# Folding an image's normalisation into the projection's weights and a bias, and a third buffer for a tile, in a four-layer scan and attention kernel

## The chip, the core and the metric

The kernel runs on one core of one Trainium2 chip. The core has five engines that run beside each other, each in its own program order: TensorE (PE; loads of its stationary operand are shown as PEld), VectorE (DVE), ScalarE (ACT), GpSimd (POOL) and SyncE (SP), which here only issues DMAs. The metric is the device time of one execution, in microseconds (us); lower is better.

## The reference

The input is four images of 64 x 64 positions with 96 channels. Layers 0 and 1 are a two-dimensional selective scan; layers 2 and 3 are linear attention and a quantised feed-forward network on the tokens. The change lies in layers 0 and 1. Cut to what matters, such a layer is:

```python
def _gn(v, G=32, eps=1e-5):                    # one mean and variance per image and group of 3 channels
    ...
    return ((g - m) / jnp.sqrt(s + eps)).reshape(v.shape)
...
xz = jnp.einsum('bhwc,ec->bhwe', x, in_proj_w)           # x is _gn(x)
xx, z = jnp.split(xz, 2, axis=-1)
xc = jax.lax.conv_general_dilated(xc, conv_w, (1, 1), [(1, 1), (1, 1)], ..., feature_group_count=E) + conv_b
xc = jax.nn.silu(xc)
xs = jnp.stack([x_hw, x_wh, x_hw[..., ::-1], x_wh[..., ::-1]], axis=1)
x_dbl = jnp.einsum('bkdl,kcd->bkcl', xs, x_proj_weight)
dts, Bmat, Cmat = jnp.split(x_dbl, [R, R + N], axis=2)
delta = jax.nn.softplus(jnp.einsum('bkrl,kdr->bkdl', dts, dt_projs_weight) + dt_projs_bias)
# scan over 4096 positions in 4 directions: h = exp(delta * A) * h + delta * B * u;  y = sum_n C * h
# then a layer norm, times silu(z), the projection out_proj_w, and the residual
```

## The kernel before, in words

`body` runs four phases, each one layer for a pair of images: layer 0 for pairs 0 and 1, then layer 1 for pairs 0 and 1. After them `token_layers` does layers 2 and 3. A phase has three parts.

- `prepare` (L151) computes everything the scan reads and writes it to DRAM: `delta` (split into three bf16 parts), `du` (delta times u), `bc` (B and C) and `ud` (u times the sum of Ds).
- `scan_phase` (L469) runs the scan, in an order written out by hand, from those DRAM tiles.
- `finish` (L546) puts the four directions together, normalises, gates, projects and adds the residual.

`run` (L699) runs `prepare` of one phase beside `finish` of the phase before: both are generators, and for each `yield` of `prepare`, `ph.beside` steps of `finish` are taken (1.0, then 0.6, then 1.25). The first `prepare` has no `finish` beside it. The scan of a phase uses all eight PSUM banks and starts when both are through. Outside `scan_phase` nothing is ordered by hand: a scheduler orders each engine's instructions from the program order, its dependences and the buffers that come free, and tile pools hand out the buffers (`bufs` of a tile says how many; a new tile waits for the oldest one's last reader).

Inside `prepare`:

- The statistics of both images come first (L186 to L209). `ph.gs[:, i]` holds, for image `i` and each of 96 channels, the mean of its group (column 0) and one over the standard deviation (column 1).
- `convolve` (L231) runs for image 0 alone, and then, as the generator `other`, for image 1 beside the `steps` of image 0. It goes over two halves `h` of the 192 inner channels. For each half it takes eight slices of the image: load of `rawi` (L242, two buffers, 96 x 512), the normalisation in place on DVE (L247: subtract the mean, multiply by the scale), the projection on PE (L251) into a PSUM bank named `c` (two buffers, shared with `steps`), and the eviction by ACT (L254) into the padded image `xp`, which has one buffer. Then eight chunks of a 3 x 3 depthwise convolution: tap 0 on ACT (L266), taps 1 to 8 on DVE (L268), and Silu with a bias on ACT (L271). Then `xu` (L276) is written to `ud` (L282). The margin of `xp` is set to zero (L239).
- `steps` (L284) runs for both images `i`, eight chunks `c` and two directions `k`, so 32 times in a preparation. Each time PE projects the 96 x 512 chunk (L291), ACT evicts it (L294 and L295), and PE projects to delta for two items, the direction forwards and backwards (L308, PSUM tile `d`, two buffers). Then for each of the two items: ACT takes Softplus into `dl` (L316) and casts it to bf16 (L317); DVE multiplies by u into `du_sb` (L318) and subtracts the cast from `dl` (L319); POOL casts the rest (L322); DVE subtracts that (L323). The results leave by the DMAs of L321 (two copies of `du`) and L324 (`parts` to `delta`). The tiles `dl`, `parts` and `du_sb` have two buffers each, from the pool `steps`.

All DMAs are issued by SP, in order. The lines that the change touches are L235 to L257 and L313.

Of the kernel before, what the change touches and what calls it, by code (L numbers as in the profile page):

```python
# [9 lines left out]
F32 = mybir.dt.float32  # L10
# [3 lines left out]
AF = mybir.ActivationFunctionType  # L14
ALU = mybir.AluOpType
# [7 lines left out]
C = 96  # L23
E = 192
# [5 lines left out]
TC = 512  # L30
# [25 lines left out]
def scan_view(t, k, c):  # L56


    part, half = t.ap[0], t.ap[1]
    if k == 0:  # L60
        off, steps = TC * c, (HW, 1)
    elif k == 1:
        off, steps = ROWS * c, (1, HW)
    elif k == 2:
        off, steps = L - 1 - TC * c, (-HW, -1)
    else:
        off, steps = L - 1 - ROWS * c, (-1, -HW)
    return bass.AP(t.tensor, t.offset + off, [part, half, [steps[0], ROWS], [steps[1], HW]])


def view(t, off, *dims):

    return bass.AP(t.tensor, t.offset + off, [t.ap[0]] + [list(d) for d in dims])


def rows(t):

    if len(t.shape) == 2:
        return t.rearrange("p (r w) -> p r w", w=HW)
    return t.rearrange("p h (r w) -> p h r w", w=HW)  # L80
# [50 lines left out]
class Scans:  # L131
# [99 lines left out]
    def convolve(self, ph, i, x, xc, in_w, taps, conv_b, dsum):  # L231


        nc = self.nc
        with self.tc.tile_pool(name="conv", bufs=1) as cp:  # L235
            for h in range(2):
                xp = cp.tile([C, PAD, PAD], F32, name="xp")
                for edge in (xp[:, 0, :], xp[:, PAD - 1, :], xp[:, 1 : PAD - 1, 0], xp[:, 1 : PAD - 1, PAD - 1]):
                    nc.vector.memset(edge, 0.0)  # L239
                for hl in range(8):  # L240
                    raw = cp.tile([C, TC], F32, name="rawi", bufs=2)
                    nc.sync.dma_start(  # L242
                        raw.rearrange("c (a p) -> c a p", p=64), x[:, hl * 8 : hl * 8 + 8, i]
                    )
                    if hl % 2 == 0:
                        yield
                    nc.vector.tensor_scalar(  # L247
                        raw, raw, ph.gs[:, i, 0:1], ph.gs[:, i, 1:2], ALU.subtract, ALU.mult
                    )
                    ps = self.bank()  # L250
                    nc.tensor.matmul(  # L251
                        ps[:C], in_w[:, h * C : (h + 1) * C], raw, start=True, stop=True
                    )
                    nc.scalar.copy(  # L254
                        view(xp, (1 + hl) * PAD + 1, (1, 8), (8 * PAD, 8), (8, 8)),
                        ps[:C].rearrange("c (a h w) -> c a h w", a=8, h=8),
                    )  # L257
                for c in range(NC):
                    yield
                    acc = xc[:, h, c * TC : (c + 1) * TC]  # L260
                    for tap in range(9):
                        dy, dx = divmod(tap, 3)
                        src = xp[:, ROWS * c + dy : ROWS * (c + 1) + dy, dx : dx + HW]
                        w = taps[:, h, tap : tap + 1]
                        if tap == 0:
                            nc.scalar.activation(rows(acc), src, AF.Copy, scale=w)  # L266
                        else:
                            nc.vector.scalar_tensor_tensor(  # L268
                                rows(acc), src, w, rows(acc), ALU.mult, ALU.add
                            )  # L270
                    nc.scalar.activation(acc, acc, AF.Silu, bias=conv_b[:, h : h + 1])  # L271
                for hl in range(8):
                    if hl % 2 == 0:
                        yield
                    xu = cp.tile([C, 8, 64], F32, name="xu", bufs=2)
                    nc.scalar.activation(  # L276
                        xu.rearrange("c w (a b) -> c w a b", b=8),
                        view(xc[:, h], hl * HW, (1, 8), (8 * HW, 8), (8, 8)),
                        AF.Copy,
                        scale=dsum[:, h : h + 1],  # L280
                    )
                    nc.sync.dma_start(ph.ud[:, h, 8 * hl : 8 * hl + 8, i], xu)  # L282

    def steps(self, ph, sp, xc, xp, dt_w, i, k, c):  # L284


        nc, cst = self.nc, self.cst
        u = scan_view(xc, k, c)
        ps = self.bank()
        for h in range(2):  # L290
            nc.tensor.matmul(rows(ps[:XD2]), xp[:, k, h], u[:, h], start=h == 0, stop=h == 1)  # L291
        xd = sp.tile([XD2, TC], F32, name="xd")

        nc.scalar.activation(xd[:XD], ps[:XD], AF.Identity, bias=cst.one_row[:XD])  # L294
        nc.scalar.activation(  # L295
            xd[64:], view(ps[64:XD2], TC - 1, (-1, TC)), AF.Identity, bias=cst.one_row[64:]
        )
        yield
        both = []
        for back in range(2):  # L300
            at = 64 * back
            g, cc = 2 * (k + 2 * back) + i, NC - 1 - c if back else c
            nc.sync.dma_start(ph.bc[cc][:, g], xd[at : at + 2 * NS])
            both.append((g, cc, scan_view(xc, k + 2 * back, cc), self.p_d.tile([C, 2, TC], F32, name="d")))
        for m in range(2):
            for back, (_, _, _, ps) in enumerate(both):
                part = slice(64 * back + 2 * NS, 64 * back + XD)
                nc.tensor.matmul(  # L308
                    ps[:, m], dt_w[part, k, m * C : (m + 1) * C], xd[part], start=True, stop=True
                )  # L310
        yield
        for g, cc, u, ps in both:
            delta = sp.tile([C, 2, TC], F32, name="dl")  # L313
            parts = sp.tile([C, NP16, 2, TC], BF16, name="parts")
            du = sp.tile([C, 2, TC], F32, name="du_sb")
            nc.scalar.activation(delta, ps, AF.Softplus)  # L316
            nc.scalar.copy(parts[:, 0], delta)  # L317
            nc.vector.tensor_tensor(rows(du), rows(delta), u, ALU.mult)  # L318
            nc.vector.tensor_tensor(delta, delta, parts[:, 0], ALU.subtract)  # L319
            for copy in range(2):  # L320
                nc.sync.dma_start(ph.du[cc][copy, g, :E].rearrange("(h e) t -> e h t", h=2), du)  # L321
            nc.gpsimd.tensor_copy(parts[:, 1], delta)  # L322
            nc.vector.tensor_tensor(parts[:, 2], delta, parts[:, 1], ALU.subtract)  # L323
            nc.sync.dma_start(  # L324
                ph.delta[cc][g].rearrange("n (h q) t -> q (n h) t", h=2),
                parts.rearrange("q n h t -> q (n h) t"),
            )
            yield
# [660 lines left out]
```

## Time and profile before

Three runs took 11978.79, 11985.35 and 12007.12 us; the median is 11985.35 us. The profile is of one more execution.

| what | value |
|---|---|
| the profiled execution's own time | 11973.68 us |
| its span, first to last instruction | 11971.9 us |
| mean granted TensorE clock | 0.826 of full speed |
| busy DVE / PE / POOL / ACT / PEld | 10052.3 / 8659.6 / 7465.3 / 7321.2 / 4597.6 us |
| first preparation | 0 to 725 us |
| the three other preparations, with a finish beside each | 2595 to 3465, 5310 to 6180, 8030 to 8900 us |
| the four scans | 725 to 2595, 3465 to 5310, 6180 to 8030, 8900 to 10769 us |
| last finish and the token layers | 10769 to 11972 us |

How to read the lines that follow. A group is: line, engine, operation, output <- input with shapes, count | busy us, mean ns of one | idle us of that engine just before these instructions, and what ended that idle time. A timeline row is: start us, duration us, engine, line, operation, output <- input, count of merged instructions, and in brackets how long the engine had been idle and what released it. A row of windows is a stretch, its length and the busy time of each engine in it. An fp32 matmul is two records on PE. Engine names with a q (SPq, DVEq) are the engine's queue: instructions that only issue or wait.

The granted clock in the preparations is 0.64 to 0.66 on the mean, in the scans 0.90 to 0.91. GpSimd is nearly idle in a preparation: 107 us of work in the first.

### The profile page before, as it was taken

The page shows a single profiled execution, that of the slowest core. Times are in us where ns is not written, and L with a number is a line of the kernel's source. Part 1 is how long each engine was busy: PE and PEld are TensorE (multiplying, and loading weights), DVE is VectorE, ACT ScalarE, POOL GpSimd, SP SyncE. Part 2 cuts the span into 40 slices and gives each one's busy share as a digit, 9 for nine tenths or more (in the row PEclk, how much of TensorE's full clock was granted, in tenths as well). Part 3 has the DMA queues.
Part 4 walks back from the last instruction along what each step waited for, and adds up shares of the span by engine and source line. Part 5 has one row for each costly group of instructions (what it writes and reads, how often), then busy time and mean ns, then how long its engine had stood idle before and what let it go on. Part 6 is the DMA issues. An engine that isn't in the chain of part 4 may idle for free.

```text
span 11971.9 us, 337755 instructions
## 1 busy us (share of the span) xinstructions
PE 8659.6 (72%) x144960; PEld 4597.6 (38%) x144960; DVE 10052.3 (84%) x10351; ACT 7321.2 (61%) x12109; POOL 7465.3 (62%) x2316
## 2 busy tenths in 40 slices
PE   3567777765767777765777777766677777777777
PEld 1124444442334444442334444433234444444333
DVE  6679999987769999987769999986769999993667
ACT  4556666655556666655556666654557666662556
POOL 0169999960149999970149999970139999990000
PEclk8579999986679989886679999986668999998887
DMA  3677777764677777765677777764677777763110
GB/s 98 185 244 254 255 252 252 252 206 138 197 231 255 254 256 257 257 216 143 193 226 256 258 257 252 258 219 136 199 221 258 255 254 250 254 232 125 18 21 11
DMA packets 952267, 2501.23 MB, mean 209 GB/s; under 512 B 324494, under 2 KB 607220, under 8 KB 819316
## 3 DMA queue, kind: packets, MB, share of 16 engines
q1 hardware_dynamic: 950772, 2479.63, 62.8%
q8 instruction: 1142, 18.71, 0.7%
q14 instruction: 353, 2.89, 0.1%
HBM read 1965.42 MB, written 513.80 MB: 207 GB/s over the span
## 4 chain that ended last, share of the span: by engine, by line
DMA 56%; PE 12%; DVE 11%; SPq 10%; ACT 5%; issue 4%; POOL 2%; POOLq 0%; DVEq 0%; ACTq 0%
DMA h<-du 52%; SPq L399 9%; DVE xc L268 4%; PE f L594 2%; POOL parts L322 2%; PE d L308 1%; PE c L291 1%; DVE parts L323 1%; DVE dl L319 1%; DVE du_sb L318 1%; DMA yk<-y 1%; PE c L251 1%; PE f L603 1%; PE f L674 1%; PE f L660 1%
## 5 line engine op out<-in xcount | busy, mean ns | idle before, releaser
L409 POOL TENSOR_TENSOR h<-h,b 128x1536 f32<-128x1536 f32 x2048 | 7021.1, 3461 | 533.5 <-DMA h<-du 191.9
L426 DVE TENSOR_TENSOR_SCAN h<-a,carry,h 128x512 f32<-128x512 f32 x5376 | 6345.7, 1259 | 174.6 <-POOL h L409 171.9
L419 ACT ACTIVATE a<-a,a_col 128x512 f32<-128x512 f32 x6144 | 4031.0, 664 | 1856.7 <-PE a L415 1830.9
L444 PEld LDWEIGHTS y<-h,cw 128*32 128x32 f32 x131072 | 2786.7, 128 | 3501.2 <-issue 1310.9
L444 PE MATMUL y<-h,cw 128*32 128x48 f32 x131072 | 3660.1, 266 | 527.3 <-DVE h L426 211.6
L415 PE MATMUL a<-dlt,rep 72*128 72x512 bf16 x6144 | 2526.8, 422 | 1302.3 <-DVE h L426 1212.9
L322 POOL CAST parts<-dl 96x1024 bf16<-96x1024 f32 x256 | 416.1, 1630 | 2793.0 <-DVE dl L319 2587.0
L456 ACT COPY d<-y 128x384 f32<-128x384 f32 x2048 | 979.8, 478 | 475.0 <-PE y L444 429.8
L426 DVE TENSOR_TENSOR_SCAN h<-a,h 128x512 f32<-128x512 f32 x768 | 868.3, 1200 | 165.5 <-ACT a L419 142.6
L415 PEld LDWEIGHTS <-rep 72*128 72x128 bf16 x6144 | 487.2, 98 | 829.0 <-issue 587.8
L308 PE MATMUL d<-xd,dt_w 7*96 7x512 f32 x1024 | 631.7, 905 | 237.5 <-ACT dl L316 149.6
L268 DVE SCALAR_TENSOR_TENSOR xc<-xp,conv_w,xc 96x512 f32<-96x512 f32 x1024 | 713.8, 756 | 54.8 <-ACT xc L266 38.9
L826 POOL MEMSET tn<- 1x4096 f32 x8 | 27.8, 3507 | 862.3 <-PE pa L846 515.1
L316 ACT ACTIVATE dl<-d 96x1024 f32<-96x1024 f32 x256 | 258.4, 1018 | 449.5 <-DVE parts L323 429.1
L318 DVE TENSOR_TENSOR du_sb<-dl,xc 96x1024 f32<-96x1024 f32 x256 | 416.2, 1633 | 116.7 <-ACT dl L316 73.0
L291 PE MATMUL c<-xc,x_proj 96*103 96x512 f32 x512 | 452.3, 1024 | 82.1 <-ACT xc L271 42.7
L594 PE MATMUL f<-yk,perm 128*128 128x384 f32 x1024 | 429.6, 564 | 95.4 <-DMA yk<-y 72.8
L251 PE MATMUL c<-rawi,in_w 96*96 96x512 f32 x256 | 206.0, 915 | 397.0 <-DVE rawi L247 312.1
L319 DVE TENSOR_TENSOR dl<-dl,parts 96x1024 f32<-96x1024 f32 x256 | 309.6, 1217 | 210.8 <-ACT parts L317 209.3
L323 DVE TENSOR_TENSOR parts<-dl,parts 96x1024 bf16<-96x1024 f32 x256 | 329.1, 1292 | 160.4 <-POOL parts L322 158.0
L308 PEld LDWEIGHTS d<-xd,dt_w 7*96 7x96 f32 x1024 | 171.8, 222 | 642.9 <-ACT dl L316 229.7
L361 ACT ACTIVATE cw<-c,gmask 128x256 f32<-128x256 f32 x512 | 286.0, 570 | 116.4 <-DMA dlt<-delta 58.1
(116 smaller groups left out, 5802.0 us busy)
## 6 DMA issues: line engine op xcount, KB each, us to landing
h<-du SPq DMA_DIRECT2D x1024, 768.0 KB
h<-du SPq DMA_DIRECT2D x2048, 384.0 KB
du<-du_sb SPq DMA_DIRECT2D x512, 384.0 KB
delta<-parts SPq DMA_DIRECT2D x256, 576.0 KB
dlt<-delta SPq DMA_DIRECT2D x512, 288.0 KB
y<-d SPq DMA_DIRECT2D x2048, 48.0 KB
yk<-y SPq DMA_DIRECT2D x256, 384.0 KB
ud<-xu SPq DMA_DIRECT2D x128, 192.0 KB
```

The source lines that it names most:

```text
L268: nc.vector.scalar_tensor_tensor(rows(acc), src, w, rows(acc), ALU.mult, ALU.add)
L291: nc.tensor.matmul(rows(ps[:XD2]), xp[:, k, h], u[:, h], start=h == 0, stop=h == 1)
L308: nc.tensor.matmul(ps[:, m], dt_w[part, k, m * C : (m + 1) * C], xd[part], start=True, stop=True)
L322: nc.gpsimd.tensor_copy(parts[:, 1], delta)
L399: self.nc.sync.dma_start(u.h[32 * first : 32 * (first + quarters), e : e + n].rearrange("p e t -> p (e t)"), source.rearrange("a g e t -> ...
L409: self.nc.gpsimd.tensor_tensor(h, h, b, ALU.mult)
L415: self.nc.tensor.matmul(u.a[n], self.cst.rep[:, h], u.dl[:, e], start=True, stop=True)
L419: self.nc.scalar.activation(u.a[n], u.a[n], AF.Exp, scale=u.ph.a_col[:, at : at + 1])
L426: self.nc.vector.tensor_tensor_scan(u.h[:, n], u.a.pop(n), u.h[:, n], 0.0 if u.c == 0 else u.ph.carry[:, at : at + 1], ALU.mult, ALU.add,)
L444: self.nc.tensor.matmul(view(u.y[32 * j : 32 * j + 32], l2 * EB, (8 * EB, 4), (1, EB)), u.ph.cw[u.c][:, l1, 8 * j + l2], view(u.h, 64 * l1 ...
L456: self.nc.scalar.copy(u.d[:, :, :, l1], u.y[:, : 32 * EB].rearrange("p (t h x) -> p t h x", t=4, h=2))
L594: nc.tensor.matmul(ps[:, : 4 * C].rearrange("p (w v e) -> p w v e", w=4, v=nv), cst.perm[:, k], view(t, off, (sw if k < 2 else -sw, 4), (1 ...
```

## The change

For each image `convolve` now first makes a scaled copy of the projection's weights, `in_ws`: row c (an input channel) times the scale of channel c. The mean's share is computed once: the scaled weights times the vector of means, on PE, one column for each half, negated on DVE into `shift`. The slices are no longer normalised: PE projects the loaded slice as it is with the scaled weights, and ACT's eviction adds `shift` as a per-partition bias (Identity with a bias in place of a copy). The tile `dl` gets three buffers in place of two, which takes another 4 KB of each of its partitions. `finish` still normalises its own slices for z (L652) as before.

```diff
         with self.tc.tile_pool(name="conv", bufs=1) as cp:
+            gs = ph.gs[:, i]
+            scaled = cp.tile([C, E], F32, name="in_ws")
+            nc.vector.tensor_scalar_mul(scaled, in_w, gs[:, 1:2])
+            shift = cp.tile([C, 2], F32, name="shift")
+            for h in range(2):
+                ps = self.bank()
+                nc.tensor.matmul(
+                    ps[:C, :1], scaled[:, h * C : (h + 1) * C], gs[:, 0:1], start=True, stop=True
+                )
+                nc.vector.tensor_scalar_mul(shift[:, h : h + 1], ps[:C, :1], -1.0)
             for h in range(2):
                 xp = cp.tile([C, PAD, PAD], F32, name="xp")
...
-                    nc.vector.tensor_scalar(
-                        raw, raw, ph.gs[:, i, 0:1], ph.gs[:, i, 1:2], ALU.subtract, ALU.mult
-                    )
                     ps = self.bank()
                     nc.tensor.matmul(
-                        ps[:C], in_w[:, h * C : (h + 1) * C], raw, start=True, stop=True
+                        ps[:C], scaled[:, h * C : (h + 1) * C], raw, start=True, stop=True
                     )
-                    nc.scalar.copy(
+                    nc.scalar.activation(
                         view(xp, (1 + hl) * PAD + 1, (1, 8), (8 * PAD, 8), (8, 8)),
                         ps[:C].rearrange("c (a h w) -> c a h w", a=8, h=8),
+                        AF.Identity,
+                        bias=shift[:, h : h + 1],
                     )
...
-            delta = sp.tile([C, 2, TC], F32, name="dl")
+            delta = sp.tile([C, 2, TC], F32, name="dl", bufs=3)
```

In the changed program every later line number is higher by 9 (L251 is L258, L254 is L261, L308 is L317, L316 is L325, L317 is L326, L323 is L332). The order of instructions in the two built programs, which tells no times, differs on the engines in `prepare`: where both convolutions are through, ACT had for each step two evictions and then Softplus, cast, Softplus, cast; now it has two evictions, cast, Softplus, Softplus, cast. The built programs hold 273 and 270 loads of ACT's tables. The order on DVE in that place is the same in both, and so is every engine's order in the scans.

## The prediction

> **What bounds the kernel now.** I read the chain that ended last, then the windows by stage, then the groups by line, and at last the timeline of two stretches of the first preparation. All times are in us.
>
> The page's chain, by engine and by line:
>
> ```profile
> DMA 56%; PE 12%; DVE 11%; SPq 10%; ACT 5%; issue 4%; POOL 2%; POOLq 0%; DVEq 0%; ACTq 0%
> DMA h<-du 52%; SPq L399 9%; DVE xc L268 4%; PE f L594 2%; POOL parts L322 2%; PE d L308 1%; PE c L291 1%; DVE parts L323 1%; DVE dl L319 1%; DVE du_sb L318 1%; DMA yk<-y 1%; PE c L251 1%; PE f L603 1%; PE f L674 1%; PE f L660 1%
> ```
>
> The 52% is the scan, and the change doesn't touch it. What it touches (L247, L251, L254, L316 to L323) lies in `prepare`. The windows cut the span into the first preparation, a scan, and the second preparation (each row: the stretch, its length, busy time of PE, PEld, DVE, ACT, POOL, clock, DMA share, GB/s):
>
> ```profile
> 0.00:725.00 725.00, 360.50 (x462) 98.17 (x463) 462.58 (x535) 325.33 (x359) 106.58 (x69) 0.66 0.56 158
> 725.00:2595.00 1870.00, 1433.72 (x34042) 811.47 (x34041) 1801.76 (x1533) 1286.54 (x2285) 1754.91 (x512) 0.91 0.72 251
> 2595.00:3465.00 870.00, 561.05 (x1678) 263.53 (x1679) 573.24 (x804) 423.17 (x519) 106.71 (x67) 0.66 0.61 175
> ```
>
> No engine is full in a preparation: DVE, the busiest, works 64% and 66%. So a preparation is made of dependences, and the four of them (725 and three of 870) are 3335 of 11972. That is the field.
>
> **The rows to cost with.** The removed normalisation and the eviction that gets a bias:
>
> ```profile
> L254 ACT COPY xp<-c 96x512 f32<-96x512 f32 x128 | 140.5, 1111 | 222.8 <-PE c L251 222.5
> ...
> L247 DVE TENSOR_SCALAR rawi<-rawi,gs 96x512 f32<-96x512 f32 x128 | 68.0, 539 | 166.5 <-DMA rawi<-in_x 98.6 <-DMA rawi<-x 67.2
> ```
>
> 128 instructions go, 68.0 of DVE time, and with them 166.5 in which DVE stood at L247 for a load while later work queued behind. The eviction stays at 128, and so do its wait for PE and its writes.
>
> **Normalisation, first image (nothing of `steps` runs yet).** First preparation, up to 62.6: the projection goes in rounds of two, each a load of 2.4 to 2.5, L247 0.55, PE 2.0, because `rawi` has two buffers. Three reloading rounds lose 0.55 + 0.1: 1.9. The first matmul, at 40.96, stands behind L247, which stands on DVE behind the statistics of the other image; it can start at about 38 once the weights are scaled: 3. Two L247 at 102 and 103 sit between the taps (L268), which DVE issues without a gap: 0.9. Between the halves (104.7 to 131.9, DVE nearly idle) the chain passes `xu`, its stores, the last `rawi` load (3.3), L247 (0.56), PE (2.0). The first two projections no longer wait for DVE, and the built program issues one more `rawi` load ahead of the `xu` stores: between 0.6 and 5.9 (a whole round), I take 4. Sum 10. In the other three, the first projection waits for nothing but the scale (no gain) and SP issues the last `rawi` loads late: 1.5 in the rounds, 1.1 in the taps, 4.4 between the halves (0.5 + 0.5 + 0.5 of L247 on the chain and half a round): 7 each.
>
> **Normalisation, second image (beside `steps`).** Here L247 costs more than its 0.54, since it queues on DVE behind the delta work. From the timeline of the first preparation:
>
> ```profile
> 217.34 3.16 DVE L323 TENSOR_TENSOR parts<-dl,parts 96x1024 bf16<-96x1024 f32 x2 [0.94 <-POOL parts L322]
> 220.43 0.99 DVE L247 TENSOR_SCALAR rawi<-rawi,gs 96x512 f32<-96x512 f32 x2
> 221.06 1.99 PE L251 MATMUL c<-rawi,in_w 96*96 96x512 f32 x2 [8.60 <-DVE rawi L247]
> ...
> 239.75 0.99 DVE L247 TENSOR_SCALAR rawi<-rawi,gs 96x512 f32<-96x512 f32 x2
> 240.39 1.99 PE L251 MATMUL c<-rawi,in_w 96*96 96x512 f32 x2 [10.46 <-DVE rawi L247]
> ```
>
> PE waits 8.6 and 10.5 for an L247 behind L318, L319 and L323. Without it PE needs only the load, and the taps, for which DVE idles 8.2 just before 229.7, start earlier by at most those 19. Late is then the load, the two PSUM banks and the eviction. Bounds: 16 x 0.54 = 8.6 if only DVE time counts, 35 if the second half gains as much as the first. I take 19. In the other three, finish work fills PE and DVE (PE waits for L247 62 in all in that stage, against 128 in the first), so 12 each.
>
> **Added work.** For each image two matmul pairs of one column (row L198: 0.30 a record, so 1.2), one scaling of 96x192 (row L338, 128x192: 0.24) and two negations (row L208: 0.15). The scaling waits for the statistics and stands ahead of the taps on DVE only when DVE idles (194 in the first preparation). PE holds the projection behind the two pairs: 1.0 a preparation on the path, inside the 3 above. The first eviction also waits for its negation, ready before ACT has finished the statistics (39.9), so nothing queued behind it on ACT is held. The eviction's bias is a pointer: row L295 with one, 39x512 from PSUM, 0.682; row L681 without, 96x512, 0.582. So +0.1 each, 3.2 of ACT a preparation; ACT is 45% to 49% busy there, and about 1 is on the path between halves, inside the 4. If ACT's cover were gone, 128 x 0.1 = 13. Table loads in the built programs: 273 and 270, 4 less ACT time, nothing on the path.
>
> **The third `dl` buffer.** Where both convolutions are done (about 500 to 700), a step with its two items A and B:
>
> ```profile
> 629.20 1.04 ACT L317 CAST parts<-dl 96x1024 bf16<-96x1024 f32 x1
> 629.22 3.72 PE L308 MATMUL d<-xd,dt_w 7*96 7x512 f32 x4 [0.47 <-ACT dl L316]
> 630.27 1.22 DVE L319 TENSOR_TENSOR dl<-dl,parts 96x1024 f32<-96x1024 f32 x1 [1.08 <-ACT parts L317]
> ...
> 633.56 1.22 DVE L323 TENSOR_TENSOR parts<-dl,parts 96x1024 bf16<-96x1024 f32 x1 [0.93 <-POOL parts L322]
> ...
> 634.88 1.02 ACT L316 ACTIVATE dl<-d 96x1024 f32<-96x1024 f32 x1 [4.64 <-DVE parts L323]
> ...
> 636.86 1.22 DVE L319 TENSOR_TENSOR dl<-dl,parts 96x1024 f32<-96x1024 f32 x1 [2.08 <-ACT parts L317]
> ...
> 639.27 1.22 DVE L323 TENSOR_TENSOR parts<-dl,parts 96x1024 bf16<-96x1024 f32 x1 [1.19 <-POOL parts L322]
> 640.42 1.91 DVE L318 TENSOR_TENSOR du_sb<-dl,xc 96x1024 f32<-96x1024 f32 x1
> 640.59 1.02 ACT L316 ACTIVATE dl<-d 96x1024 f32<-96x1024 f32 x1 [2.47 <-DVE parts L323]
> ```
>
> The period is one closed loop: L319 to L323 of A 4.51, Softplus and cast 2.08, L319 to L323 of B 3.63, Softplus and cast 2.22; sum 12.44, and 13.12 in every other step, where L318 reads u across rows (1.9 in place of 1.22). ACT issues Softplus, cast, Softplus, cast. In the built changed program it issues cast of A, two Softplus, cast of B: the cast of A no longer stands behind a Softplus, but the cast of B still does, behind one that takes the buffer freed by A's L323. So 2.08 stays, and 2.22 becomes the L318 it had covered (1.25 or 1.94): 24.3 in place of 25.6 for two steps, 0.62 a step. 14 steps: 9 in the first preparation; in the others, with finish work between, 6 each. Earlier, where L316 waits for L323 too (45 of 156 in the first), 3 and 2.
>
> Next late would be PE: eight L308 records at 0.93 and four L291 at 0.93, 11.2 a step, at a granted clock of 0.50:
>
> ```profile
> 560.00:620.00 60.00, 52.08 (x57) 13.67 (x58) 38.52 (x29) 24.60 (x29) 15.72 (x10) 0.50 0.78 227
> ```
>
> The Trainium skill (TensorE: Matmul & The Clock Gate, Part 1) says the clock is binary and that some 3.4 us of sustained work raise it to full. By that rule PE's step would cost 5.6 and could bind nothing. The row disagrees: 87% busy, 7.4 on end at 629 to 636, and 0.50 throughout. I keep 11.2. DMA, 0.78 busy at 12.8, has its floor at 10.
>
> **Sum.** First preparation 10 + 19 + 9 + 3 = 41; the others 7 + 12 + 6 + 2 = 27, three times 81: 122 in all. The profiled execution took 11973.7 (span 11971.9); less 122, 11851.7. The median of the runs is 11.7 above it: 11863.
>
> **Rivals.** (1) *The loops open wider*: the delta loop falls to PE's 11.2 (1.6 a step in place of 0.62, over 14 x 4 steps 55 more) and the second image reaches its upper bound (40 more): 11768. For it, the idle engines; against it, the built order on ACT. 15%. (2) *It was hidden anyway*: loads, SP's order and finish work are as late as L247 was, and only the first image's gains and some DVE time remain, 45: 11940. For it, 166.5 of L247's idle time was a load's doing. 18%. (3) *Slower, by ACT's new order*: B's cast now stands behind the second Softplus, which needs the last L308 of its step; where PE is late, each step's DVE chain starts one L308 pair and one Softplus later, 1.86 + 1.02 = 2.9. It decides once PE ends L308 after A's L323. PE is full for long in the last three preparations (100% of 3248 to 3276). Half of some 78 such steps cost 113, less 76 for the convolution: 12022. Against it, PE's loop (10.96) is shorter than 12.2 where I can follow it. 10%.
>
> **Numbers.** The forecast has 57%. The measurement tells 0.3% (36) from no change, so faster ends at 11949. Faster: 57 - 2, 15, and 10 of the second rival's 18: 0.80; same: 0.12; slower: 0.08. The range 11765 to 11955 leaves out the slower rival, the low half of the first, and the top of the second.
>
> **What would show it.** Right: L251 (L258) never waits for DVE, the gap between the halves of the first image falls from 27 to about 23, the taps of the second image start before 230, Softplus in pairs every 12.2, the scans unchanged at 1845 to 1870. Wrong: L258 waiting as long for its load, casts waiting behind Softplus, or a period still at 12.8, or PE's clock rising in the steps.

## The result, and the profile after

Four runs of the changed kernel took 11874.15 to 11923.01 us, median 11887.4; four of the kernel before 11978.79 to 12007.12, median 11984.52. The ratio is 0.9918 (95% interval 0.9898 to 0.9937): 97 us less, where 122 were forecast. A second measurement, with the kernel before taken again beside it, gave 0.9905 (0.9892 to 0.9919). The profiled execution is the slowest of the four (11923.01), 51 below the profiled one of before, since its scans are 42 longer in sum. A scan is counted from its first to its last multiplication by B on POOL (L418, L409 before), and a preparation is what lies ahead of it:

| profiled execution | preparations | sum | scans | sum |
|---|---|---|---|---|
| before | 725.0, 866.2, 862.7, 867.5 | 3321.4 | 1870, 1856, 1850, 1866 | 7443 |
| after | 710.2, 837.6, 838.6, 842.5 | 3228.9 | 1880, 1871, 1869, 1866 | 7485 |

The preparations lost 92.5, about what the medians say. The scans, which the change leaves as they were, took 7443 to 7512 in the 14 profiled executions of this study, and before's is the lowest. So I compare preparations, and use the medians for totals.

The chain of the changed kernel, by engine and by line:

```profile
DMA 57%; PE 12%; DVE 11%; SPq 10%; ACT 5%; issue 3%; POOL 2%; POOLq 0%; DVEq 0%; ACTq 0%
```

It is the same chain: the scan's loads. The windows show where the time went: the first preparation, a scan, and the second preparation:

```profile
0.00:710.00 710.00, 327.87 (x470) 99.14 (x471) 446.50 (x509) 327.46 (x359) 104.38 (x68) 0.65 0.58 161
710.00:2590.00 1880.00, 1437.56 (x34042) 811.68 (x34041) 1802.49 (x1533) 1288.62 (x2285) 1754.98 (x512) 0.90 0.72 250
2590.00:3428.00 838.00, 537.95 (x1686) 260.89 (x1687) 555.18 (x778) 422.89 (x517) 109.78 (x66) 0.65 0.63 181
```

The groups, kept apart by shape, of the lines that were L251, L254, L316 and L317:

```profile
L326 ACT CAST parts<-dl 96x1024 bf16<-96x1024 f32 x256 | 265.4, 1041 | 146.8 <-DMA delta<-parts 145.6
L325 ACT ACTIVATE dl<-d 96x1024 f32<-96x1024 f32 x256 | 257.7, 1018 | 348.6 <-DVE parts L332 259.2 <-PE d L317 87.2 <-DVE xo L696 1.2
L258 PE MATMUL c<-rawi,in_ws 96*96 96x512 f32 x256 | 195.5, 874 | 241.3 <-ACT xp L261 101.6 <-DMA rawi<-in_x 84.5 <-DMA rawi<-x 48.0
L261 ACT ACTIVATE xp<-c,shift 96x512 f32<-96x512 f32 x128 | 152.5, 1205 | 140.3 <-PE c L258 139.8
```

The projection had stood idle 312.1 for L247; now it stands 101.6 for the eviction and 132.5 for its loads (48.2 before). Softplus waited 429.1 for L323; now 259.2 for the same and 87.2 for PE. The cast's wait for the stores of `parts` rose from 99.2 to 145.6. The bias costs 94 ns an eviction (1111 to 1205), the 0.1 of the forecast.

Where each preparation gained, from the taps' and the delta work's instructions in the trace. The taps are the nine products of the convolution. Each column is the change of a stage's own length, after less before, with the forecast in brackets; the 3 and the 2 that the forecast gave to earlier steps of the `dl` loop stand with the second image. The last stage runs to the scan's first multiplication:

| preparation | to the end of the first image's taps | second image's taps | from there to the last L332 | tail | sum |
|---|---|---|---|---|---|
| first | -7.4 (forecast -10) | +0.8 (-22) | -9.3 (-9) | +1.2 | -14.7 |
| second | -7.0 | -24.8 | +3.1 | +0.1 | -28.6 |
| third | -3.5 | -20.7 | +2.1 | -2.0 | -24.1 |
| fourth | -6.4 | -23.5 | +6.3 | -1.4 | -25.0 |
| mean of these three | -5.6 (-7) | -23.0 (-14) | +3.8 (-6) | -1.1 | -25.9 (-27) |

The first preparation fell short by 26. The others met their 27, but from other terms than I summed. One execution's columns carry a few us of chance: in a second profiled execution of the changed kernel the +3.8 was -0.4.

### The profile page after: what moved, and what is told of

Its sections match the earlier page's. It is cut to its first block, busy times and chain, and to the rows that moved or that the text cites. A ratio compares the mean times of both kernels' runs of the same rounds, so it can differ in the third digit from the quotient of the medians.

```text
span 11921.2 us, 337611 instructions
## 1 busy us (share of the span) xinstructions
PE 8549.8 (72%) x144992; PEld 4586.7 (38%) x144992; DVE 9991.8 (84%) x10247; ACT 7335.1 (62%) x12106; POOL 7480.2 (63%) x2316
## 4 chain that ended last, share of the span: by engine, by line
DMA 57%; PE 12%; DVE 11%; SPq 10%; ACT 5%; issue 3%; POOL 2%; POOLq 0%; DVEq 0%; ACTq 0%
DMA h<-du 53%; SPq L408 9%; DVE xc L277 4%; PE f L603 2%; POOL parts L331 2%; PE d L317 1%; DVE dl L328 1%; PE f L683 1%; PE c L300 1%; DVE du_sb L327 1%; PE f L694 1%; DVE parts L332 1%; DMA yk<-y 1%; PE f L669 1%; PE f L612 1%
## 5 line engine op out<-in xcount | busy, mean ns | idle before, releaser
L418 POOL TENSOR_TENSOR h<-h,b 128x1536 f32<-128x1536 f32 x2048 | 7020.9, 3461 | 574.0 <-DMA h<-du 229.6
L317 PE MATMUL d<-xd,dt_w 7*96 7x512 f32 x1024 | 532.0, 885 | 263.6 <-ACT dl L325 141.2
L327 DVE TENSOR_TENSOR du_sb<-dl,xc 96x1024 f32<-96x1024 f32 x256 | 409.9, 1607 | 123.6 <-ACT dl L325 67.2
L325 ACT ACTIVATE dl<-d 96x1024 f32<-96x1024 f32 x256 | 257.7, 1018 | 348.6 <-DVE parts L332 259.2
L332 DVE TENSOR_TENSOR parts<-dl,parts 96x1024 bf16<-96x1024 f32 x256 | 326.2, 1280 | 170.0 <-POOL parts L331 168.8
L317 PEld LDWEIGHTS d<-xd,dt_w 7*96 7x96 f32 x1024 | 160.0, 216 | 586.5 <-ACT xd L303 200.1
L258 PE MATMUL c<-rawi,in_ws 96*96 96x512 f32 x256 | 195.5, 874 | 241.3 <-ACT xp L261 101.6
```

What stands on the lines that cost most here:

```text
L317: nc.tensor.matmul(ps[:, m], dt_w[part, k, m * C : (m + 1) * C], xd[part], start=True, stop=True)
L418: self.nc.gpsimd.tensor_tensor(h, h, b, ALU.mult)
```

## The experiments

All figures are ratios to the kernel before on the same chip, from five rounds, with an interval of 0.0012 to 0.0016 to each side (0.001 is 12 us). "Preparations" is the sum of the four in the profiled execution; before it is 3321. No kernel leaves work out.

| kernel | ratio (median, us) | preparations | the first |
|---|---|---|---|
| changed kernel again | 0.9905 (11903) | 3217 | 709 |
| fold alone | 0.9955 (11963) | 3266 | 722 |
| three `dl` alone | 0.9943 (11954) | 3258 | 712 |
| changed, 3 `rawi` | 0.9876 (11873) | 3174 | 685 |
| changed, `rawi` loads on GpSimd | 0.9851 (11839) | 3146 | 678 |
| the same, no fold | 0.9889 (11881) | 3181 | 688 |
| 4 `dl`, no fold | 0.9920 (11915) | 3225 | 702 |
| changed, loads on GpSimd, 3 `rawi` | 0.9846 (11835) | 3137 | 669 |
| the same, no fold | 0.9838 (11824) | 3130 | 675 |
| changed, loops of L317 exchanged | 0.9946 (11944) | 3254 | 727 |
| 3 `dl`, 3 `rawi`, no fold | 0.9912 (11911) | 3215 | 692 |
| fold, loads on GpSimd, 4 `dl` | 0.9804 (11775) | 3099 | 666 |

**The parts alone.** The fold without the buffer, and the buffer without the fold:

```diff
-            delta = sp.tile([C, 2, TC], F32, name="dl", bufs=3)
+            delta = sp.tile([C, 2, TC], F32, name="dl")
```

> The fold alone; dl keeps its two buffers. By the prediction's sum the fold was worth 86 of the 122 (29 in the first preparation, 19 in each other) and this is 86 below the kernel before. My theory after the result: in the second image L258 got the load to wait for in place of L247, the fold keeps only the first image's gain (7 in the first preparation, the taps of the second image at most 8 earlier) and this is 40 to 65 below the kernel before. Rival: the two parts need each other, and alone each brings under 25.

> The third dl buffer alone; the normalisation stays on DVE. By the prediction 36 below the kernel before (12 in the first preparation, 8 in each other), with a step of 12.2 in place of 12.8 where both convolutions are through. My theory after the result: 9 in the first preparation, 10 to 15 in each other, 35 to 55 below. Rival: with L247 still between the delta work on DVE, the buffer brings under 20.

The fold brings 54 (forecast 86; my second guess, 40 to 65, holds), the buffer 68 (forecast 36; above my second guess of 35 to 55). Alone they add up to 122; together they gave 97 and 114, which the intervals do not tell from 122. The preparations, at 55 and 63 alone and 92 and 104 together, say that the parts overlap somewhat. In the first preparation the fold brings 2.6 and the buffer 12.8. The fold's first image ends 8 earlier there, and its second image then takes 4 longer than before. That is the term to explain.

**What took L247's place.** The timeline of the changed kernel at the start of the second image, first preparation, the same place as the prediction's rows from 217 to 240 (the last row below is of the kernel before):

```profile
221.07 1.99 PE L258 MATMUL c<-rawi,in_ws 96*96 96x512 f32 x2 [1.11 <-DMA rawi<-in_x]
...
226.31 0.30 SPq L333 DMA_DIRECT2D delta<-parts  x1
...
229.86 0.55 SPq L333 DMA_DIRECT2D delta<-parts  x1
...
230.50 9.43 SPq L252 DMA_DIRECT2D rawi<-in_x  x3
237.60 1.99 PE L258 MATMUL c<-rawi,in_ws 96*96 96x512 f32 x2 [14.54 <-DMA rawi<-in_x]
...
240.87 8.13 DVE L277 SCALAR_TENSOR_TENSOR xc<-xp,conv_w,xc 96x512 f32<-96x512 f32 x12 [9.63 <-ACT xp L261]
...
243.56 6.80 DVE L268 SCALAR_TENSOR_TENSOR xc<-xp,conv_w,xc 96x512 f32<-96x512 f32 x10 [2.81 <-ACT xp L254]
```

The row of 237.60 is the eighth slice of the half. Its buffer is that of the sixth, whose matmul ended at 211.3, so SP could have issued its load then; but the stores of L330 and L333 stand ahead of it in SP's order and wait for the delta work on DVE and POOL. SP issued the load at 230.50, and PE got the slice at 237.60; why it was 7.1 on its way isn't settled. In the kernel before, the load went out at 228.54, the matmul ran at 240.39, and it seemed to have waited 10.46 for L247. The second image's first tap on DVE came at 229.7 in both kernels; it doesn't need the eighth slice. The taps that do started at 240.87, with DVE idle 9.63 for that slice's eviction, against 243.56 before: of the 10.46, 2.7 were gained. Two ways to take the load out of that place, a further buffer, or another queue with the same buffers:

```diff
-                    raw = cp.tile([C, TC], F32, name="rawi", bufs=2)
+                    raw = cp.tile([C, TC], F32, name="rawi", bufs=3)
```

> The changed kernel with a third rawi buffer, so that a load can be issued a slice ahead, before SP reaches the stores that it stood behind. Theory (the load is what is late next in the second image): L258's wait for loads, 133 in all in the changed kernel, falls below 60, the second image's taps of the first preparation start 5 to 15 earlier, and the time is 15 to 45 below the changed kernel. Rival (the delta work on DVE and ACT sets the pace beside the second image, the load only fills its gaps): within 10 of the changed kernel.

```diff
-                    nc.sync.dma_start(
+                    nc.gpsimd.dma_start(
                         raw.rearrange("c (a p) -> c a p", p=64), x[:, hl * 8 : hl * 8 + 8, i]
                     )
```

> The changed kernel with the rawi loads issued by GpSimd's queue in place of SP's, buffers as they are: a load then waits for its buffer and for GpSimd's casts (L331), not for the stores that stand ahead of it on SP. Theory (SP's order holds the load): as with a third buffer, 15 to 45 below the changed kernel. Rival 1 (the load isn't what limits): within 10. Rival 2: the loads' waits hold GpSimd's casts of the delta work behind them, and the kernel is 10 to 40 above the changed one.

Both are faster than the changed kernel: 0.0029 to 0.0042 below it, or 35 to 50, and 0.0054 to 0.0067, or 65 to 80, by its two measurements. The queue's gain is above the range I gave. The first preparation loses 24 and 31 more, and its second image's first tap comes at 207.9 and 216.8. With the third buffer that is 22 earlier, where I had thought 5 to 15; 9 of it come from the first image, whose rounds of loads it shortens as well. The row for the GpSimd queue:

```profile
210.82 0.78 POOL L252 DMA_DIRECT2D rawi<-in_x  x1
...
213.10 1.34 PE L258 MATMUL c<-rawi,in_ws 96*96 96x512 f32 x2
```

The issue takes 0.78 of GpSimd between two casts, and L258 no longer waits for the load. One expectation failed: with three buffers L258's wait for loads didn't fall below 60, it was 184. 129 of that are four waits of 30 to 33, one in each preparation, between the halves of the second image (the changed kernel has one there too, of 29.20). SP's rows of that kernel in the first preparation show the reason:

```profile
327.87 1.38 SPq L333 DMA_DIRECT2D delta<-parts  x1
...
337.03 4.11 SPq L330 DMA_DIRECT2D du<-du_sb  x2
341.25 0.59 SPq L333 DMA_DIRECT2D delta<-parts  x1
341.94 10.14 SPq L252 DMA_DIRECT2D rawi<-in_x  x4
```

The last four loads of the next half stand behind the stores, however many buffers are free; PE gets the first at 349.75. With the loads on GpSimd that sum is 57, and the gap between those halves of the first preparation falls from 55 (328.6 to 383.9) to 30 (311.9 to 341.5). The Trainium skill (DMA: Bandwidth & Descriptors, "Issuing engine by pattern") gives simple loads to SP, and calls the path that SP uses generally faster. The trace agrees: in the first image's rounds PE waits 1.0 to 1.2 for SP's loads and 1.9 to 2.0 for GpSimd's. Here the place in the queue's order mattered more than the path.

**Is the fold worth more once the load is out of the way?** Kernels without the fold beside those with it:

> The kernel before with the third dl buffer and with its rawi loads on GpSimd's queue; no fold. Beside the run that has the fold as well (0.985 of the kernel before) it gives the fold's worth with the load out of the way. Theory: the fold's gain was taken up by the load's place in SP's order, so without that place it is worth about what the prediction's sum said, 86 (29 in the first preparation, 19 in each other), and this kernel is at 0.991 to 0.993. Rival: the loads by GpSimd bring their gain by themselves, with L247 or without; then this kernel is at 0.987 to 0.989, and the fold is worth 50 or less here too.

> The kernel before with three dl buffers, the rawi loads on GpSimd's queue and three rawi buffers; no fold. It stands beside the kernel that has all this and the fold (0.9846 of the kernel before; first preparation 669). With the load well ahead, PE's waits for L247 are all DVE's. If L247 behind the delta work is then what is late, the fold is worth more here than the 45 that it was worth with two rawi buffers: 60 to 90, this kernel at 0.990 to 0.992. If the convolution's taps on DVE are the limit of the second image, L247 costs little more than its own time: the fold is worth 20 to 45, this kernel at 0.986 to 0.9885.

> The kernel before with three dl and three rawi buffers, all loads on SP; no fold. With the loads on GpSimd and three rawi buffers the fold was worth nothing (0.9838 without it, 0.9846 with it). If a third rawi buffer does the same as the fold (both take L247 out of the round of load, normalisation, projection and next load), this kernel is where the same with the fold is, 0.986 to 0.989, and below the changed kernel (0.9905 to 0.992). If the loads' place on SP was the reason, the fold keeps its 50 here and this kernel is at 0.9905 to 0.993.

(With `dl` at three buffers throughout.)

| loads, `rawi` buffers | without the fold | with the fold | the fold is worth |
|---|---|---|---|
| SP, 2 | 0.9943 | 0.9918, 0.9905 | 30, 46 |
| SP, 3 | 0.9912 | 0.9876 | 43 |
| GpSimd, 2 | 0.9889 | 0.9851 | 46 |
| GpSimd, 3 | 0.9838 | 0.9846 | -10 |

The difference of two ratios is known to about 0.002 (24 us). My theory wanted 86 in the third row and had to fall: the fold stayed at 46, as the rival said. For the fourth row I had thought 60 to 90 or 20 to 45, and it is nothing or a small loss. The last run's first theory (a third buffer does the same as the fold) failed too, at 0.9912 where it wanted 0.986 to 0.989; the other, that the fold keeps its worth there, held. What fits all four rows, though no run isolates it, is this: the fold shortens the wait for a slice, and it is worth what of that wait is left on the path. The second preparation goes with it. With GpSimd and two buffers the second image's first tap comes at 234.7 with the fold and 257.5 without; with three buffers at 234.5 and 235.0. And the fold did not shorten the taps themselves: with two buffers the two stretches of them take 214 with the fold and 199 without, and of the 23 only 13 are left at the preparation's end. These are windows of the kernel with the fold, loads on GpSimd and two `rawi` buffers in its first preparation, the stretches of the second image's taps with the gap between its halves:

```profile
250.00:330.00 80.00, 42.99 (x51) 11.21 (x50) 68.61 (x76) 48.45 (x51) 19.57 (x15) 0.52 0.60 170
330.00:350.00 20.00, 18.17 (x26) 5.63 (x26) 9.72 (x9) 16.20 (x20) 2.57 (x3) 0.66 0.82 226
350.00:450.00 100.00, 48.69 (x72) 15.42 (x72) 95.91 (x100) 60.92 (x64) 24.30 (x13) 0.52 0.62 178
```

DVE (the third busy time of a row) is 86% and 96% busy in the two stretches. I take it that a removed L247 is worth little more than its own 0.54 there; no run shows that alone. Why the fold costs 1 to 6 in each later preparation of the fourth row is open.

**The buffer's loop.** In the changed kernel, where both convolutions are through:

```profile
596.03 1.22 DVE L332 TENSOR_TENSOR parts<-dl,parts 96x1024 bf16<-96x1024 f32 x1 [0.93 <-POOL parts L331]
597.35 1.02 ACT L325 ACTIVATE dl<-d 96x1024 f32<-96x1024 f32 x1 [4.09 <-DVE parts L332]
598.27 1.03 ACT L326 CAST parts<-dl 96x1024 bf16<-96x1024 f32 x1
...
599.33 1.22 DVE L328 TENSOR_TENSOR dl<-dl,parts 96x1024 f32<-96x1024 f32 x1 [2.08 <-ACT parts L326]
599.94 4.43 PE L317 MATMUL d<-xd,dt_w 7*96 7x512 f32 x8 [3.36 <-ACT xd L303]
...
602.89 1.91 DVE L327 TENSOR_TENSOR du_sb<-dl,xc 96x1024 f32<-96x1024 f32 x1
```

It is the loop that the prediction wrote down. A's L332 frees the buffer, Softplus and cast of B follow, DVE stands its 2.08, and where it stood 2.22 there is now L327. A step takes 12.16 (eight steps, read at L332), against 12.78; 24.3 for two steps was forecast. Was the 2.08 there for the reason given? A fourth buffer, with no fold so that it fits, and the same order on ACT:

```diff
-            delta = sp.tile([C, 2, TC], F32, name="dl")
+            delta = sp.tile([C, 2, TC], F32, name="dl", bufs=4)
```

> The kernel before with four dl buffers and no fold; the order on ACT is cast, Softplus, Softplus, cast, as with three. The prediction said that 2.08 of the loop stays since the cast of B stands behind a Softplus that takes the buffer freed by A's L323. With a fourth buffer that Softplus takes one that has long been free. If that was the reason, the step falls from 12.2 to between 10.3 and 11.4 where both convolutions are through, and the time is 25 to 65 below the kernel with three buffers (0.9943 of the kernel before). Rival: the casts wait for the stores of parts, which has two buffers, and the step stays within 0.2 of 12.2. If PE needed 11.2 for a step, as the prediction took it, the step ends at no less than 11.2.

```profile
592.14 1.04 ACT L317 CAST parts<-dl 96x1024 bf16<-96x1024 f32 x1 [4.09 <-DMA delta<-parts]
593.21 1.93 ACT L316 ACTIVATE dl<-d 96x1024 f32<-96x1024 f32 x2
...
596.84 1.04 ACT L317 CAST parts<-dl 96x1024 bf16<-96x1024 f32 x1 [1.70 <-DMA delta<-parts]
...
598.52 4.43 PE L308 MATMUL d<-xd,dt_w 7*96 7x512 f32 x8 [3.03 <-ACT xd L294]
```

It was. Both Softplus run on end with no wait of their own, and the step is 11.04 over eight steps (single ones 10.15), below the 11.2 that I had given PE. The casts now wait for the stores of `parts`, the next limit. The whole gained 0.0023 over three buffers (28, though the intervals touch). The idle 3.03 of PE before L308 says that PE isn't full at 11.04.

**PE's floor.** In the kernel before four records of L308 (the two matmuls of one item) took 3.72 at a granted clock of 0.50; in the changed one the eight of both items take 4.43 at the same clock. A step is then 3.74 + 4.43 = 8.2 of PE, not 11.2. I tried to undo what I thought the cause:

```diff
-        for m in range(2):
-            for back, (_, _, _, ps) in enumerate(both):
+        for back, (_, _, _, ps) in enumerate(both):
+            for m in range(2):
```

> The changed kernel with the two loops around L317 exchanged: the four matmuls of an item follow each other (rows 16 to 22 of xd for the one, 80 to 86 for the other) instead of taking turns. In the changed kernel eight records take 4.43 where the granted clock is 0.50, in the kernel before four take 3.72. If matmuls on different rows of the array run beside each other and those on the same rows do not, eight take 7.2 to 7.5 here, and a step's PE work is 11.2 again. If the cause is something else (the wait for a PSUM buffer between the fours), they take 4.4 to 4.8. Either way the step stays at 12.2 and the time within 20 of the changed kernel (0.9905 to 0.992 of the kernel before), since PE isn't the bound; should PE bind, the step would rise above 12.4.

```profile
607.80 0.68 ACT L303 ACTIVATE xd<-c,one_row 39x512 f32<-39x512 f32 x1
...
608.53 4.43 PE L317 MATMUL d<-xd,dt_w 7*96 7x512 f32 x8 [4.97 <-ACT xd L303]
...
609.24 0.53 PEld L317 LDWEIGHTS d<-xd,dt_w 7*96 7x96 f32 x3 [0.32 <-ACT xd L304]
...
612.29 1.02 ACT L325 ACTIVATE dl<-d 96x1024 f32<-96x1024 f32 x1 [3.10 <-PE d L317]
613.33 1.04 ACT L326 CAST parts<-dl 96x1024 bf16<-96x1024 f32 x1
```

The edit took effect: in the built program PE has both matmuls of one item and then both of the other, as the kernel before has them in these steps; the changed kernel has them in turns. The eight still take 4.43, so taking turns in the program isn't the cause. The starts of the eight records, here and in the changed kernel, form two series, each spaced 0.85 to 0.96 as before's four were, the second 0.71 behind the first. The weight load at the head of the second series (609.24) waits for L304, which writes the second item's rows of `xd` and comes 0.70 behind L303. So the second series is the second item's, and the two run beside each other. That they can because each has its own rows of the array (32 to 38 and 96 to 102 by the kernel's slices, not those of the expectation) is what the Trainium skill has (TensorE: Matmul & The Clock Gate, Part 3: matmuls on different tiles of the array run concurrently); no run here put both on the same rows. In the kernel before the second item waited for its PSUM buffer (0.47 for L316 in the prediction's rows) behind the late Softplus, and started after the first had ended.

The run showed something else. With the exchange the scheduler went back to before's order on ACT, Softplus, cast, Softplus, cast, and three buffers in that order give a step of 13.42, longer than before. It isn't that PE is full: PE idles 4.97 before L317, for an L303 that stands on ACT behind the late cast. The time (0.9946) is 34 to 49 above the changed kernel, not within 20. So a third buffer in the old order gained nothing in this run; it pays by the order on ACT that it lets the scheduler choose. (The run changed PE's order with ACT's, and the two are not told apart.)

**Together.** Loads on GpSimd with three `rawi`, and then the best of it all: the fold, loads on GpSimd, four `dl`, and, for room, the weights loaded afresh into `in_ws` for each image and scaled in place:

> The changed kernel with its rawi loads on GpSimd's queue and a third rawi buffer. Each alone stood at 0.985 and 0.988. Theory: both remove the same wait, so together they give at most 20 more than the loads on GpSimd alone: 0.983 to 0.985. Rival: they remove different waits and add up, 0.981 or less.

```diff
-            nc.vector.tensor_scalar_mul(scaled, in_w, gs[:, 1:2])
+            nc.gpsimd.dma_start(scaled, in_w)
+            nc.vector.tensor_scalar_mul(scaled, scaled, gs[:, 1:2])
...
-            delta = sp.tile([C, 2, TC], F32, name="dl", bufs=3)
+            delta = sp.tile([C, 2, TC], F32, name="dl", bufs=4)
```

> A combination of what the runs showed: the fold, the rawi loads on GpSimd's queue, and four dl buffers (the copy of the projection's weights is loaded afresh for each image into in_ws and scaled in place, which makes the room). Four buffers instead of three brought 0.0023 without the fold and 1.1 a step in the first preparation. If that adds to the loads' gain, 0.981 to 0.984; a step of 11.0 where both convolutions are through, and the first preparation near 668. If the output stores limit what is left, no more than 0.002 is gained over 0.985.

With the fold a third `rawi` adds no more than 6 to the GpSimd loads (0.9846), as if both removed the same wait; without the fold it adds 61 (0.9889 to 0.9838). The last kernel is the fastest of the study: 11775, 0.9804 (0.9791 to 0.9818), just below the range I gave; its step is 11.4 (11.0 forecast) and its first preparation 666.

## Why the prediction was right, and where it was not

- **The time**: 11887 against 11863, 24 slower than forecast and well inside the range. That it came so near is partly luck. By the preparations of the two kernels with one part each, the fold was worth 55 (86 forecast), the buffer 63 (36 forecast), and both together 92 and 104: a term too high, one too low, and an overlap of 14 to 26 that I had left out.
- **First image**: 10 and 7 forecast, 7.4 and 5.6 measured. The gap between the halves fell from 27.3 to 21.4 (23 forecast). L258 waits for DVE only 14.9 in all, for the statistics. Right.
- **Second image, first preparation: the step that failed.** "PE waits 8.6 and 10.5 for an L247 behind L318, L319 and L323. Without it PE needs only the load", and "I take 19". It needs the load, and the load was no nearer: L258 waits 14.54 for it, and the stage got 0.8 longer; with the fold alone it got 4.1 longer. The trace names the last releaser; L247 was the last of several that were all late. I named the load as next late and didn't price it by SP's order, though the order of the stores ahead of it was there to be read. The two-sided bound, 8.6 to 35, should have reached to nothing.
- **Second image, the others**: 12 for the fold and 2 for the buffer forecast, 23.0 measured. Alone, the fold takes 17.8 off that stage and the buffer 7.5. I had cut the fold's term because finish work fills PE and DVE, and it gained more there, not less; but 6.4 of the fold's 17.8 are lost again in the next stage.
- **The loop of `dl`**: 24.3 for two steps, 24.32 measured; the reason of the 2.08 is shown by the fourth buffer. In the first preparation 9.3 for 9. In the others the buffer alone takes 7.4 off the stretch after the convolutions (6 forecast), but with the fold that stretch got 3.8 longer: some of what the second image gains is given back there. The trace shows with what: beside the shorter second image less of `finish` fits. In each of these preparations some 468 of its records on PE fell into the stretch after the convolutions before, 480 with the buffer alone and 520 in the changed kernel, where they take 10 to 13 more than before.
- **PE as the next bound**, 11.2 a step: wrong; 8.2, and a step of 11.04 was reached. The clock did stay at 0.50 in the steps (520 to 680), so the row was right against the clock rule. What was wrong was to take the duration of one item, measured where the other had to wait, twice for both.
- **The rivals.** Hidden anyway (11940): its mechanism, a load as late as L247, is what happened, in one preparation of four. Slower by ACT's new order: the reverse; the new order is what pays. (The 76 that this rival took off for the convolution should have been the sum's 86.) Wider loops: only with a fourth buffer and the loads moved.
- **The tests I set**: first taps "before 230" was no test, since before had them at 229.7. The casts of A do wait (1.2 to 1.4, for a store), off the path. The scans of the profiled execution (1866 to 1880) left my 1845 to 1870, without a cause in the change.

## What to carry to other kernels

An idle time put down to one engine's instruction is worth what the next latest input leaves of it: before pricing its removal, find when each other input could have come, and for a load that is when the issuing queue gets past the waits ahead of it. On one in-order DMA queue, loads for the next work behind stores of the last make prefetching as late as the stores; moving them to an idle engine's queue brought here 65 to 80 us. And a buffer's worth may lie in the order it lets a scheduler choose, so read the built order before trusting the count.

## What the runs showed that was not expected

- Four matmuls of 7 rows (eight records) took 4.43 where two (four records) took 3.72, at the same granted clock of 0.50: two items' matmuls that need not wait for each other cost far less than twice one's.
- Stages that no edit touched varied more than some of the effects: the four scans took 7443 to 7512 in 14 profiled executions. An effect under 1% was read at the stage that it touches.
